# Mask and maximum of a neighbourhood attention in one VectorE instruction, and one activation table for gelu and tanh

## The chip, the cores and the metric

The kernel runs on one core of a Trainium2 chip. A core has TensorE (PE, with its weight loads shown apart), VectorE (DVE), ScalarE (ACT), GpSimd (POOL) and SyncE (SP), which issues the DMAs here. Each engine runs its own queue in order and waits for the others by semaphores. The metric is the device time of one execution in microseconds (us).

## The reference

Four layers follow one another on an input of 4 images of 128 channels, 64 x 64 pixels, all in float32: a deformable neighbourhood attention, a recurrence over the 4096 pixels, a stack of eight state-space layers (mamba), and a mixture of experts. The change lies in the first. Cut to what matters there:

```python
q = conv1x1(x, Wq, bq)
o = dwconv(q_off, off_dw_w, off_dw_b, K // 2)          # 7 x 7, by channel
o = gelu(ln2d(o, ln_w, ln_b), approximate=False)
off = tanh(einsum('bchw,oc->bohw', o, off_pw_w)) * rng
xs = grid_sample_zeros(x, off + ref)                   # offsets below one pixel
k, v = conv1x1(xs, Wk, bk), conv1x1(xs, Wv, bv)
logits = einsum('bhwgc,bhiwjgc->bhwgij', qh * SCALE, kb)   # 7 x 7 neighbours
attn = softmax(logits.reshape(B, H, W, G, K * K), -1)
out = einsum('bhwgij,bhiwjgc->bhwgc', attn, vb) + lepe
return conv1x1(out, Wo, bo)
```

The result is added to the input, and the recurrence behind it starts from a batch normalization over all of it, so it can't begin before the last block of the attention layer is done.

## The kernel before

An image is cut into 8 blocks of 512 pixels (8 rows), 32 blocks in all. A block is cut into 4 tiles of 128 queries; a tile's keys lie in a window of 14 x 22 = 308 pixels, and a mask of 0 and -1e30 leaves each query its own 7 x 7 of them. There are 4 heads to a tile.

`conv_layer` writes the order of all engines out by hand, as a software pipeline. Its loop runs over rounds `i` from -2 to 36. In a round, block `i` has the 49 taps of the 7 x 7 convolution, block `i - 1` the offset branch behind it (pieces named `o.`), block `i - 3` its attention, and blocks further back and ahead the output projection (`w.`), the next layer's first product (`v.`) and the projection to q (`q.`). Rounds 3 to 31 have both taps and attention; rounds 32 to 34 have attention without taps.

A round has 8 steps `s`, each with one pair of heads. In a step the calls are issued in this order, and each engine keeps its part of it:

1. on odd steps, PE's products with the values of the tile before (`values`); on even steps `weighed` (VectorE, L451, multiplies by the softmax's shares `ts`), the reciprocal of `share` (L423) and GpSimd's copies of the window;
2. PE transposes the two exps of the step before (`turn`, L411);
3. for each head of the pair: `masked` (VectorE, L393: logits in PSUM plus mask, to `lg` in SBUF), one tap, `largest` (VectorE, L396: the negated maximum of `lg`, to `top`), one tap, `exp` (ScalarE, L400, with `top` as its bias and the sum as its accumulator output), and `keep` (ScalarE, L419, moves a transposed exp out of PSUM);
4. on odd steps ScalarE's copies `ts` (L445) and `vk` (L374);
5. the pieces of `CPLAN`'s row left of the bar;
6. the logits of the next pair (PE, L380, two banks of PSUM, so each waits until `masked` has read the bank);
7. the rest of the step's taps;
8. `POOL_TAPS[s]` taps on ScalarE (`last_tap`: L291 multiplies, GpSimd adds in L293);
9. the pieces right of the bar.

Of the 49 taps, 39 run on VectorE (`tap`, L279; the first is L272), 3, 5, 4, 7, 6, 8, 4 and 2 of them in the eight steps. Each reads the accumulator that the one before it wrote. The other 10 run on ScalarE and GpSimd: 1 in step 1, 4 in step 4, 3 in step 5 and 2 in step 7.

In step 2 stands the offset branch: `o.norm` (L235, VectorE), `o.gelu` (L296, ScalarE), two matmuls `o.off0` and `o.off1` (L307, PE), and `o.tanh` (`fractions`: two tanh in L315, each followed by a GpSimd instruction, L316, from which the sampling of step 3 goes on). [...] Everything else in the layer uses the set with exp and ln, so `gelu` ends with a request for that set (L297) and `fractions` does too (L318); the gelu and the tanh each have a load of their own ahead of them. The profile counts these loads under L296, L297, L315 and L318.

Of the kernel before, what the change touches and what calls it, by code (L numbers as in the profile page):

```python
# [11 lines left out]
ALU = mybir.AluOpType  # L12
AX = mybir.AxisListType

EXP_LN = "natural_log_exp_and_others"
# [19 lines left out]
NKEY = KR * KC  # L35
# [75 lines left out]
CPLAN = """  # L111
w.fetch f.fetch | o.cen
o.var | o.rstd
w.rpe0 o.norm | o.gelu o.off0 o.off1 o.tanh
o.across0 | q.cen v.cen q.var o.across1 q.rstd w.rpe1
q.norm | o.down v.var w.rpe2 v.rstd
v.norm | v.pw w.wo v.wx
# [2 lines left out]
""".strip("\n").split("\n")  # L120

TAPS = 3, 5, 4, 7, 6, 8, 4, 2
POOL_TAPS = 0, 1, 0, 0, 4, 3, 0, 2
N_POOL = sum(POOL_TAPS)
NSTEP = 8


# [9 lines left out]
def conv_layer(tc, ops, I, x1_d, wx_d, stats):  # L137
# [7 lines left out]
    nc = tc.nc  # L145
    with ExitStack() as ctx:
        c = ctx.enter_context(tc.tile_pool(name="l0c", bufs=1))
        w = ctx.enter_context(tc.tile_pool(name="l0w", bufs=2))
# [18 lines left out]
        mask = c.tile([P, 9, NKEY], F32, name="mask")  # L167
        nc.sync.dma_start(out=mask, in_=I["mask"])

        def col(i):  # L170
            return vec[:, i : i + 1]
# [19 lines left out]
        scale = HD**-0.5  # L191
# [75 lines left out]
        def tap(o, t):  # L267

            x = shifted(o, t, K)
            if t == 0:  # L270
                o.acc = ps_c.tile([P, BLK], F32, tag="acc", name="acc")
                nc.vector.tensor_scalar(  # L272
                    rows(o.acc), x, dww[:, 0:1], col(V_DWB), ALU.mult, ALU.add
                )
                return
            to = o.acc
            if t == K * K - N_POOL - 1:
                to = o.off = w.tile([P, BLK], F32, tag="off", name="off")
            nc.vector.scalar_tensor_tensor(  # L279
                rows(to), x, dww[:, t : t + 1], rows(o.acc), ALU.mult, ALU.add  # L280
            )

        def last_tap(o, n):

            t = K * K - N_POOL + n
            by = dww[:, t : t + 1]
# [7 lines left out]

        def gelu(o):
            nc.scalar.activation(o.on, o.on, AF.Gelu, bias=col(V_LNB), scale=col(V_LNW))  # L296
            nc.scalar.preload_act_table_set(EXP_LN)  # L297

        def o_norm(o):
            o.on = w1.tile([P, BLK], F32, tag="on", name="on")  # L300
# [57 lines left out]
        def window(t):  # L358

            t.win = wins[t.n % len(wins)]  # L360
            nc.gpsimd.tensor_copy(
                t.win[:, 0:NKEY].rearrange("p (a b) -> p a b", a=KR),
                vt[:, t.r0 : t.r0 + KR, t.c0 : t.c0 + KC],
            )
# [23 lines left out]
        def masked(t, g):  # L388
            if g == 0:
                t.top = w.tile([P, G], F32, tag="top", name="top", bufs=3)  # L390
                t.tot = w.tile([P, G], F32, tag="tot", name="tot", bufs=3)
            t.lg[g] = w4.tile([P, NKEY], F32, tag="lg", name="lg")
            nc.vector.tensor_tensor(t.lg[g], t.pl[g][:, 0:NKEY], mask[:, t.m, :], ALU.add)  # L393

        def largest(t, g):
            nc.vector.tensor_reduce(t.top[:, g : g + 1], t.lg[g], AX.X, ALU.max, negate=True)  # L396

        def exp(t, g):
            t.ex[g] = exps[g]
            nc.scalar.activation(  # L400
                t.ex[g][:, 0:NKEY],
                t.lg[g],
                AF.Exp,
                bias=t.top[:, g : g + 1],
                accum_out=t.tot[:, g : g + 1],
            )

        def turn(t, g):
            t.pt[g] = bank("pt")
            for n in range(3):  # L410
                nc.tensor.transpose(  # L411
                    t.pt[g][:CHK, n * P : (n + 1) * P],
                    t.ex[g][:, n * CHK : (n + 1) * CHK],
                    ops.ident,
                )

        def keep(t, g):
            t.at[g] = w.tile([P, 3, P], F32, tag=f"at{g}", name="at")
            nc.scalar.copy(t.at[g][:CHK].rearrange("p n c -> p (n c)"), t.pt[g][:CHK, 0 : 3 * P])  # L419

        def share(t):

            nc.vector.reciprocal(t.tot, t.tot)  # L423
            t.rx = w.tile([P, G, HD], F32, tag="rx", name="rx")
            nc.gpsimd.tensor_copy(t.rx, t.tot.unsqueeze(2).to_broadcast([P, G, HD]))

        def values(t):

            t.pa = ps_a.tile([P, 4, P], F32, tag="pa", name="pa")
            for n in range(3):  # L430
                for g in range(G):
                    ch = slice(g * HD, (g + 1) * HD)
                    nc.tensor.matmul(
                        t.pa[ch, 0, :],
                        t.vk[:CHK, n, ch],
                        t.at[g][:CHK, n, :],
                        start=n == 0,
                        stop=n == 2,
                        skip_group_check=True,
                    )  # L440
            nc.tensor.transpose(t.pa[:, 1, :], t.rx.rearrange("p g d -> p (g d)"), ops.ident)

        def shares(t):
            t.ts = w.tile([P, P], F32, tag="ts", name="ts")
            nc.scalar.copy(t.ts, t.pa[:, 1, :])  # L445

        def weighed(t):
            o = t.block
            if t.j == 0:
                o.sblk = w.tile([P, ROWS, W], F32, tag="sblk", name="sblk")  # L450
            nc.vector.tensor_tensor(  # L451
                o.sblk[:, :, t.j * TC : (t.j + 1) * TC],
                rows(t.pa[:, 0, :]),
                rows(t.ts),
                ALU.mult,
            )
# [38 lines left out]
        def statistics(o):  # L495
# [12 lines left out]
            "o.rstd": lambda o: rstd(o, ops.eps6),  # L508
            "o.norm": o_norm,
            "o.gelu": gelu,  # L510
            "o.off0": lambda o: offset(o, 0),
            "o.off1": lambda o: offset(o, 1),
# [19 lines left out]
        plan = [[part.split() for part in row.split("|")] for row in CPLAN]  # L532
# [4 lines left out]
        def block(n):  # L537
            return blocks[n] if 0 <= n < NB else None

        def pair(p):  # L540

            if not 0 <= p < NB * NSTEP:
                return None
            t, h = divmod(p, 2)
            return tiles[t], (2 * h, 2 * h + 1)

        def tile_at(n):
            return tiles[n] if 0 <= n < len(tiles) else None
# [3 lines left out]
        for i in range(-2, NB + ATT + 2):  # L552
            who = {"q": block(i + 2), "o": block(i - 1), "w": block(i - 4), "v": block(i - 5)}
            who["f"] = block(i + 3)
            taken = n_last = 0

            def taps(n):

                nonlocal taken, n_tap
                while block(i) and n and n_tap:  # L560
                    tap(block(i), taken)
                    taken, n_tap, n = taken + 1, n_tap - 1, n - 1

            def do(what):
                if who[what[0]]:
                    pieces[what](who[what[0]])

            for s in range(NSTEP):
                p = NSTEP * (i - ATT) + s
                n_tap = TAPS[s]  # L570

                old = tile_at(p // 2 - 1) if p % 2 else None
                if old:
                    values(old)
                if p % 2 == 0:
                    if tile_at(p // 2 - 2):
                        weighed(tile_at(p // 2 - 2))
                    if tile_at(p // 2 - 1):
                        share(tile_at(p // 2 - 1))
                    if tile_at(p // 2):  # L580
                        window(tile_at(p // 2))
                now, was, then = pair(p), pair(p - 1), pair(p + 1)
                if was:
                    for g in was[1]:
                        turn(was[0], g)
                for k in range(2):
                    if now:
                        masked(now[0], now[1][k])
                        taps(1)
                        largest(now[0], now[1][k])  # L590
                        taps(1)
                        exp(now[0], now[1][k])
                    if was:
                        keep(was[0], was[1][k])
                if old:
                    shares(old)
                if p % 2 and tile_at(p // 2):
                    turn_window(tile_at(p // 2))
                for what in plan[s][0]:
                    do(what)  # L600
                if then:
                    logits(*then)
                taps(n_tap)
                for n in range(POOL_TAPS[s]):
                    if block(i):
                        last_tap(block(i), n_last)
                        n_last += 1
                for what in plan[s][1]:
                    do(what)


class Recurrence:
# [1059 lines left out]
```

## Time and profile before

| what | value |
|---|---|
| median of 3 runs | 15626.52 us (15621.09 to 15630.72) |
| the profiled execution | 15620.96 us |
| its span, from first to last instruction | 15619.2 us |
| instructions | 304876 |
| PE busy over the span | 92% |
| VectorE busy | 88% |
| ScalarE busy | 77% |
| GpSimd busy | 84% |

The attention layer takes the first 1655 us or so of the span: the last of its statistics, L496, is at 1653.46 us. The recurrence runs alone behind it (its first tanh is at 1665.71 us), and mamba from about 2000 us on; both are unchanged code. In the attention layer, from 0 to 1900 us, these groups are the ones that the change touches:

| line, engine, operation | count | mean ns |
|---|---|---|
| L393 VectorE, `lg` from `pl` and mask, 128x308 | 512 | 468 |
| L396 VectorE, `top` from `lg`, 128x308 | 512 | 468 |
| L279 VectorE, a tap, 128x512 | 1184 | 750 |
| L400 ScalarE, exp, 128x308 | 512 | 550 |
| L291 ScalarE, a tap, 128x512 | 288 | 731 |
| L293 GpSimd, its add, 128x512 | 288 | 1272 |
| L296 ScalarE, gelu, 128x512 | 32 | 813 |
| L315 ScalarE, tanh, 128x512 | 64 | 597 |
| table loads under L296, L297, L315, L318 | 32 each | 1283 |

How to read the rows below: a group's length is from its start to its last write, and the next instruction of the engine can start before that. In brackets stands how long the engine had been idle before an instruction, and what ended the wait. "xm L222 x4" is four passes over PE in one piece; a float32 matmul is counted as two. In the chain, each piece starts when what it waited for was done.

### The profile page before, as it was taken

What the parts mean: (1) busy time and instruction counts of PE and PEld (TensorE: products, weight loads), DVE (VectorE), ACT (ScalarE), POOL (GpSimd) and SP (SyncE); (2) the same over time, 40 slices, a digit from 0 to 9 for tenths busy, and PEclk for the clock granted to TensorE, in tenths of its full rate; (3) what the DMA queues carried; (4) which work ended last, traced back from release to release, by engine and by line L of the source; (5) the groups of instructions that cost most, each with busy time, mean ns of one, the idle gap of its engine ahead of it and who ended that gap; (6) DMA issues with size and microseconds to landing.
All of it is one profiled execution on the core that took longest, in us unless ns stands there. A gap on an engine that the chain in (4) does not pass through costs nothing.

```text
span 15619.2 us, 304876 instructions
## 1 busy us (share of the span) xinstructions
PE 14418.2 (92%) x121498; PEld 10710.3 (69%) x121498; DVE 13693.7 (88%) x14955; ACT 12010.6 (77%) x23617; POOL 13173.4 (84%) x9087
## 2 busy tenths in 40 slices
PE   6888989999999999999999999999999999989996
PEld 3444557777777777777777777777777777766665
DVE  8998159998999899989999899989998999999994
ACT  6888367887788788878788788878787888777773
POOL 4555059999999999999999999999999999999994
PEclk8999999999999999999999999999999999999998
DMA  0000012222222222222222222222222222222224
GB/s 22 22 22 20 18 70 105 100 97 105 100 104 96 104 96 105 99 103 99 101 102 96 104 98 105 98 105 96 103 101 103 98 98 105 96 102 94 102 94 178
DMA packets 423486, 1431.72 MB, mean 92 GB/s; under 512 B 204080, under 2 KB 204464, under 8 KB 290864
## 3 DMA queue, kind: packets, MB, share of 16 engines
q1 hardware_dynamic: 421920, 1411.95, 24.9%
q8 instruction: 960, 15.73, 0.4%
q14 instruction: 462, 3.78, 0.1%
q10 hardware_dynamic: 144, 0.26, 0.0%
HBM read 1353.33 MB, written 58.72 MB: 90 GB/s over the span
## 4 chain that ended last, share of the span: by engine, by line
POOL 62%; issue 11%; ACT 10%; PE 9%; DVE 7%; DMA 1%; POOLq 0%; SPq 0%; DVEq 0%; ACTq 0%
POOL hs L1063 46%; POOL hs L1035 6%; POOL dtx L953 4%; ACT dA L992 4%; DVE hs L1047 2%; DVE acc L279 2%; POOL state L1060 2%; POOL u L1128 2%; PE yT L1067 2%; POOL part L848 1%; PE f L865 1%; PE xm L222 1%; ACT L1147 1%; ACT xc L870 1%; PE dBx L1014 1%
## 5 line engine op out<-in xcount | busy, mean ns | idle before, releaser
L1047 DVE TENSOR_TENSOR_SCAN hs<-dA,state,dBx 128x512 f32<-128x512 f32 x7168 | 8717.6, 1263 | 987.9 <-PE dBx L1014 869.8
L1063 POOL TENSOR_TENSOR hs<-hs,Cb 128x2048 f32<-128x2048 f32 x2048 | 9293.5, 4538 | 165.8 <-POOL state L1060 1.6
L992 ACT ACTIVATE dA<-dt,A 128x512 f32<-128x512 f32 x7168 | 4729.3, 722 | 7.4 <-DVE hs L1047 1.2
L1067 PE MATMUL yT<-ident,hs 128*128 128x128 f32 x32768 | 4331.9, 276 | 8.9 <-POOL hs L1063 8.9
L1067 PEld LDWEIGHTS yT<-ident,hs 128*128 128x128 f32 x32768 | 3782.6, 144 | 770.8 <-issue 648.6
L1014 PE MATMUL dBx<-diag,dtxT 64*128 64x128 f32 x57344 | 4187.0, 286 | 72.1 <-DVE hs L1047 44.9
L1014 PEld LDWEIGHTS dBx<-diag,dtxT 64*128 64x128 f32 x57344 | 3511.7, 188 | 1026.7 <-issue 695.4
L688 ACT ACTIVATE z<-p 128x4 f32<-128x4 f32 x4096 | 710.5, 173 | 1451.6 <-PE p L685 1445.5
L685 PEld LDWEIGHTS p<-z,vt 128*128 128x128 f32 x8192 | 1233.2, 189 | 616.1 <-ACT z L688 357.1
L685 PE MATMUL p<-z,vt 128*128 128x4 f32 x8192 | 1463.2, 249 | 95.5 <-ACT z L688 78.0
L1035 POOL TENSOR_TENSOR hs<-Bb,dtx 128x512 f32<-128x512 f32 x1024 | 1274.8, 1280 | 5.7 <-PE yT L1067 4.7
L1047 DVE TENSOR_TENSOR_SCAN hs<-dAp,state,hs 128x512 f32<-128x512 f32 x1024 | 1228.4, 1262 | 0.0
L879 DVE SCALAR_TENSOR_TENSOR xc<-f,taps,xc 128x509 f32<-128x509 f32 (+2 forms) x1536 | 1130.7, 736 | 43.7 <-ACT tail L874 16.5
L980 DVE TENSOR_TENSOR diag<-f,i 128x512 f32<-128x512 f32 x1792 | 1158.2, 671 | 8.0 <-PE f L968 8.0
L1060 POOL COPY state<-hs 128x4 f32<-128x4 f32 x2048 | 387.5, 189 | 774.8 <-DVE hs L1047 617.6
L1147 ACT ACT_TABLE_LOAD x768 | 985.3, 1283 | 10.6
L279 DVE SCALAR_TENSOR_TENSOR acc<-qp,dww,acc 128x512 f32<-128x512 f32 x1184 | 887.5, 750 | 12.2
L992 ACT ACTIVATE dAp<-dt,A 128x512 f32<-128x512 f32 x1024 | 709.1, 692 | 209.4 <-DVE hs L1047 178.4
L894 PE MATMUL f<-u,given 128*128 128x512 f32 x1024 | 510.2, 620 | 333.0 <-ACT pos L1113 322.5
L870 ACT ACTIVATE xc<-f,edge,taps 128x1 f32<-128x1 f32 x1536 | 426.5, 350 | 438.9 <-POOL edge L855 438.3
L953 POOL TENSOR_TENSOR dtx<-dt,xc 128x512 f32<-128x512 f32 x512 | 651.2, 1272 | 12.1 <-ACT dt L947 12.1
L963 ACT COPY dtxT<-f 128x512 f32<-128x512 f32 x512 | 297.8, 582 | 385.3 <-PE f L960 385.3
(240 smaller groups left out, 16442.4 us busy)
## 6 DMA issues: line engine op xcount, KB each, us to landing
Cb<-c_d SPq DMA_DIRECT2D x1024, 1024.0 KB, 4.7
Bb<-c_d SPq DMA_DIRECT2D x256, 512.0 KB, 5.5
given<-in_m_given_dram SPq DMA_DIRECT2D x64, 640.0 KB, 6.0
slab<-in_w_dram SPq DMA_DIRECT2D x60, 512.0 KB, 9.9
x<-x_d SPq DMA_DIRECT2D x96, 256.0 KB, 4.8
c_d<-dbl SPq DMA_DIRECT2D x512, 32.0 KB, 1.6
x_d<-x SPq DMA_DIRECT2D x63, 256.0 KB, 2.2
xb<-in_x_dram SPq DMA_DIRECT2D x32, 256.0 KB, 3.1
```

What stands on the lines that cost most here:

```text
L279: nc.vector.scalar_tensor_tensor(rows(to), x, dww[:, t : t + 1], rows(o.acc), ALU.mult, ALU.add)
L685: nc.tensor.matmul(self.p[:, k, :], self.vt, self.before, start=False, stop=True, skip_group_check=True)
L879: nc.vector.scalar_tensor_tensor(x, o.v[h][:, : TL - k], taps[:, o.l, h, DC - 1 - k : DC - k], x, ALU.mult, ALU.add)
L953: nc.gpsimd.tensor_tensor(to, blocks(o.dt[h]), blocks(o.xc[:, h, :]), ALU.mult)
L980: nc.vector.tensor_tensor(o.diag[:, sp], bt.unsqueeze(2).to_broadcast([P, NB, 64, 2]), i64.unsqueeze(1).unsqueeze(3).to_broadcast([P, NB, ...
L992: nc.scalar.activation(o.dA[j][:, k, :], o.dt[h], AF.Exp, scale=A[:, o.l, h, n : n + 1])
L1014: nc.tensor.matmul(o.dBx[j][:, at : at + 64, :], o.dtxT[h][row, n, :], o.diag[row, sp, n], start=True, stop=True,)
L1035: nc.gpsimd.tensor_tensor(hs[:, k, :].rearrange("p (q n t) -> p q n t", n=NB, q=2), o.Bb[:, k, :].rearrange("p (q n t) -> p q n t", n=NB, ...
L1047: nc.vector.tensor_tensor_scan(hs[:, k, :], o.dA[j][:, k, :], hs[:, k, :] if sp == SP_B else o.dBx[j][:, :, k], state[:, o.l, o.b, h, s : ...
L1063: nc.gpsimd.tensor_tensor(hs, hs, o.Cb[f], ALU.mult)
L1067: nc.tensor.matmul(o.yT[:, n, :], x[:, n * P : (n + 1) * P], ops.ident, start=start and n == 0, stop=True, is_transpose=True, skip_group_c ...
L1147: return lambda o: nc.scalar.preload_act_table_set(name)
```

## The change

Mask and maximum: `masked` uses `tensor_tensor_reduce`, which writes `(pl + mask) * -1` to `lg` and the minimum of that over the 308 keys to `top`. So `top` holds the negated maximum as before, `lg` holds negated logits, and the exp takes a scale of -1. `largest` is gone, and where a tap stood ahead of it and one behind it, both taps now follow `masked`. In the built program the call is two instructions of VectorE, one that writes `lg` and one that writes `top`.

Tables: `gelu` no longer asks for the exp-and-ln set behind itself, and gelu and tanh use one set. Between `o.off1` and `o.tanh` stand two of ScalarE's ten taps (`p.tap`), one each taken from step 4 and step 5. They are the second and third of the ten in order, so each has its add on GpSimd ahead of L316. A block's loads go from four to two.

```diff
 w.fetch f.fetch | o.cen
 o.var | o.rstd
-w.rpe0 o.norm | o.gelu o.off0 o.off1 o.tanh
+w.rpe0 o.norm | o.gelu o.off0 o.off1 p.tap p.tap o.tanh
...
-POOL_TAPS = 0, 1, 0, 0, 4, 3, 0, 2
-N_POOL = sum(POOL_TAPS)
+POOL_TAPS = 0, 1, 0, 0, 3, 2, 0, 2
+N_POOL = 2 + sum(POOL_TAPS)
...
         def gelu(o):
             nc.scalar.activation(o.on, o.on, AF.Gelu, bias=col(V_LNB), scale=col(V_LNW))
-            nc.scalar.preload_act_table_set(EXP_LN)
...
-            nc.vector.tensor_tensor(t.lg[g], t.pl[g][:, 0:NKEY], mask[:, t.m, :], ALU.add)
-
-        def largest(t, g):
-            nc.vector.tensor_reduce(t.top[:, g : g + 1], t.lg[g], AX.X, ALU.max, negate=True)
+            nc.vector.tensor_tensor_reduce(
+                t.lg[g], t.pl[g][:, 0:NKEY], mask[:, t.m, :], -1.0, 3e38, ALU.add, ALU.min,
+                accum_out=t.top[:, g : g + 1],
+            )
...
                 bias=t.top[:, g : g + 1],
+                scale=-1.0,
                 accum_out=t.tot[:, g : g + 1],
...
                         masked(now[0], now[1][k])
-                        taps(1)
-                        largest(now[0], now[1][k])
-                        taps(1)
+                        taps(2)
                         exp(now[0], now[1][k])
...
-                for n in range(POOL_TAPS[s]):
-                    if block(i):
+                for what in ["p.tap"] * POOL_TAPS[s] + plan[s][1]:
+                    if what[0] != "p":
+                        do(what)
+                    elif block(i):
                         last_tap(block(i), n_last)
                         n_last += 1
-                for what in plan[s][1]:
-                    do(what)
```

## The prediction

> **What bounds the kernel now.** I read the windows by stage first, then the chain of waits inside the attention stage, then the timelines of VectorE and ScalarE along one round of it. The change touches only the convolution layer. Its last statistics feed the recurrence, so whatever the layer gains or loses reaches the end of the kernel one for one.
>
> ```profile
> 248.00:1530.00 1282.00, 1141.40 (x6358) 556.72 (x6358) 1160.22 (x2248) 1060.63 (x2322) 697.27 (x754) 0.95 0.07 22
> ```
>
> The columns are length, then PE, weight load, VectorE, ScalarE and GpSimd busy, then the granted clock. PE is busy 89%, VectorE 90%, ScalarE 83%: no engine is a bound alone, so I follow the chain. Here it is through the round from 817 to 859 us (start, length, what):
>
> ```profile
> 821.32 0.64 ACT exps L400 x2
> ...
> 822.34 1.28 ACT L296
> 823.64 0.82 ACT on L296
> 824.51 3.39 PE po L307 x4
> 827.92 0.60 ACT f L315
> 828.53 1.28 ACT L318
> ...
> 830.89 2.04 PE xm L222 x4
> ...
> 838.77 0.46 DVE lg L393
> ...
> 846.55 0.28 DVE sblk L451
> ...
> 855.34 0.29 DVE sblk L451
> ...
> 858.27 0.78 PE pl L380 x2
> ```
>
> It changes engine five times: VectorE until the maximum at 821.3 (A), ScalarE and PE for the offset branch until 829.8 (B), PE alone until the logits at 838.8 (C), VectorE until sblk at 846.6 (D), VectorE, then ScalarE, until sblk at 855.3 (E), VectorE until the bank of logits is free at 858.3 (F). After that PE again. The L296 loads at 535.04 and 965.54 us are nine rounds apart, so a round takes 47.8 us. VectorE and ScalarE in A and B:
>
> ```profile
> 818.73 0.47 DVE L396 TENSOR_REDUCE top<-lg 128x1 f32<-128x308 f32 x1
> 819.12 0.75 DVE L279 SCALAR_TENSOR_TENSOR acc<-qp,dww,acc 128x512 f32<-128x512 f32 x1
> 819.77 0.47 DVE L393 TENSOR_TENSOR lg<-pl,mask 128x308 f32<-128x308 f32 x1
> 820.16 0.75 DVE L279 SCALAR_TENSOR_TENSOR acc<-qp,dww,acc 128x512 f32<-128x512 f32 x1
> ...
> 825.96 3.12 DVE L279 SCALAR_TENSOR_TENSOR acc<-qp,dww,acc 128x512 f32<-128x512 f32 x4
> 831.95 0.29 DVE L451 TENSOR_TENSOR sblk<-pa,ts 128x128 f32<-128x128 f32 x1 [2.87 <-ACT ts L445]
> 832.15 0.17 DVE L423 RECIPROCAL tot<-tot 128x4 f32<-128x4 f32 x1
> ```
>
> ```profile
> 824.47 1.28 ACT L297 ACT_TABLE_LOAD   x1
> 825.76 1.28 ACT L315 ACT_TABLE_LOAD   x1
> 827.05 0.60 ACT L315 ACTIVATE f<-po 128x512 f32<-128x512 f32 x1
> 827.92 0.60 ACT L315 ACTIVATE f<-po 128x512 f32<-128x512 f32 x1 [0.27 <-PE po L307]
> ```
>
> Starts matter more than lengths: 819.12 less 818.73 says a maximum occupies VectorE for 0.39 us, the mask the same, and a tap between them 0.65. Four taps in a row take 3.12, 0.78 each: a tap waits for the accumulator that the tap before it wrote, and the attention instructions between taps hide that today. In B the loads L297 and L315 lie beside the two L307 matmuls (PE waits 2.46 us for the gelu first); the second tanh waits for PE, not for them.
>
> [...] the trace has 1283 and no drain (the gelu starts 1.30 us after its load), so I use 1.28. [...] The trace shows a granted 0.50 from 824.0 to 827.0, right after the 2.46 us wait; so these four passes take 3.4 us, where the same shape on a warm clock (L341) takes 2.0.
>
> **The change, part by part.** Per round 16 heads; 29 rounds have both heads and taps.
>
> *The fused instruction.* Removed per head 0.387 + 0.385 = 0.77 us of VectorE; added is a pair of price c. The main half does what L393 does (0.39, the same operands and length). For the read, the nearest small row is the reciprocal of four elements: 0.17 long, and the next instruction starts 0.085 after it. I take c = 0.475, the maximum being usable 0.39 + 0.16 + 0.03 = 0.58 us after the start. From below c is 0.39 (the read free), saving 0.085 more per head, 1.4 us a round of VectorE's work. From above: if the read waits for the whole 0.47 and holds the engine 0.19 (ScalarE's own accumulator read lasts 190 ns), c = 0.66. [...]
>
> *The taps after it.* They now come in twos, so the second waits: 0.13 us more. Counting steps of four or more taps twice, the three-tap and two-tap steps once: 14 times 0.13 = 1.8 us a round. VectorE's work falls by 16 x 0.295 - 1.8 = 2.9 us a round, but only A, D, E and F have it on the path:
> - A: today 3.62 us from the first mask to the second exp (817.70 to 821.32); after 0.475 + 0.78 + 0.65 + 0.58 = 2.49. Gain 1.13. ScalarE is free for that exp from 819.9, so it can use it.
> - D: 7.78 us today; two heads save 0.59, two new tap pairs cost 0.26. Gain 0.33.
> - E: VectorE alone would gain 0.95. But PE loses its wait of 0.51 for the mask before L341 and is otherwise without a gap to the last exp, so sblk comes about 0.4 earlier than what A to D give. Gain 0.4; the rest turns into waiting at L451.
> - F: 2.93 us become 2.83. Gain 0.1.
> - C is PE's and ScalarE's own, nothing. In step 3 and 4 VectorE's saving only lengthens its 2.87 us wait at L451.
>
> *Loads and moved taps.* Two of the four loads go, 2.57 us of ScalarE a round. Two taps (0.73 each, 0.65 back to back) come beside L307 in their place, one each out of steps 4 and 5, where ScalarE isn't on the chain: nothing there. Their two adds on GpSimd (1.27 each) now fall into its 9.7 us idle stretch before L316, and its offset work ends earlier. In B the path is L307, not the loads, whenever PE is at half clock (four passes 3.2 to 3.8 us): gelu's end to the last load takes about 4.0 both ways, no gain. In the five or so of 27 rounds where the clock is full (2.0 us), the loads decide today (3.7 us); after, L307 and a tanh do (2.6): gain 1.1. A moves the gelu 1.13 us earlier while PE's work before it stays, so PE's idle wait falls from 2.46 to 1.3 us and the half clock should come less often. The bottom is no gain at all in this respect (0.2 us a round on average), the top is full clock in every round: 4.0 less 2.6, 1.35. Rounds with a 0.98 us gap before o.cen's L222 run it at half clock in 11 of 27. I take 60% for L307, near its lower end: 0.45 us.
>
> *Scale.* The exp gets an immediate scale of -1 and the same bias: no cost, since L291 carries a scale from memory and fits the same rate. If that were wrong it would show as a longer L399.
>
> Sum: 1.13 + 0.45 + 0.33 + 0.4 + 0.1 = 2.4 us a round, 29 rounds, 70. The three rounds without taps are PE's chain save for two short stretches of heads (1565 to 1568, 1601 to 1604) and one offset branch: 3 us. The filling rounds without attention have only the loads: 2 us. Together 75. The profiled execution took 15620.96 us (its span 15619.2 and 1.8 around it), the median of the runs is 5.6 above it. 15620.96 - 75 = 15546; on the median's scale about 15550.
>
> **The rivals.**
> 1. Clock: PE stays warm at L307 everywhere, B gains 1.35, and half of o.cen's slow rounds (11 of 27 at 1.6 us more, 0.65 a round) go too: 2.4 + 0.9 + 0.5 = 3.8 us a round, with the 5 us 115: 15511. For it: the gap at L307 halves. Against it: o.cen is slow behind a gap of under 1 us.
> 2. Serial read: c = 0.66. A gains 0.87, B 0.45, E 0.35 at its last head, D and F lose 0.1 together: 1.5 a round, 46 in all: 15580. For it: nothing here shows an accumulator read on VectorE. Against it: ScalarE's starts 0.09 before its exp ends and lets the next begin after 0.09.
> 3. The other side: c = 0.97. Then VectorE has 3.2 + 1.8 = 5 us more a round and the path changes by A +0.17, B +0.45, D -0.66, E -0.9, F -0.7: 1.65 us lost a round, 48 in all: 15674. It takes the place of the gain from c = 0.81 on, and is worth 0.2% (31 us) from 0.91. [...]
>
> That the loads don't go isn't open: the order of the changed program has two a round.
>
> **How the numbers follow.** Forecast 0.60, clock 0.12, serial read 0.18, slower pair 0.10. A measurement of this kernel can tell about 0.2%, 31 us, from no change. Faster by more: 0.57 of the forecast's (0.03 could come out at under half), all of the clock's, two thirds of the serial read's: 0.81. Within: 0.03 + 0.06 + 0.02 = 0.11. Slower: 0.08. The range reaches from just beyond the clock case, 15508, to 15615, past the serial read; only the slower pair lies outside.
>
> **What would show it.** The pair's starts give c: next tap 0.45 to 0.5 us after the mask is right, above 0.8 is rival 3. Taps in twos at 0.78 and 0.65. Loads x64 in place of x128, the gap before L307's successor near 1.3 us, its passes at 3.4 or 2.0. L451's waits on ts longer. Rounds of about 45.4 us in place of 47.8, and the recurrence starting some 75 us earlier, with everything behind it unchanged. I am wrong if VectorE's saving is all waited away at L451, that is, if rounds shrink by under 1 us although c is below 0.5.

## The result, and the profile after

The changed kernel takes 15467.45 us (median of 4 runs, 15463.73 to 15478.33), the kernel before beside it 15623.81 us (4 runs, 15620.59 to 15630.72): a ratio of 0.990, 95% interval 0.9883 to 0.9918. That is 156 us gained where 75 were forecast, so the direction was right and the size half. The time lies 41 us under the range, and beyond the clock rival too.

All of it lies in the attention layer. The layer's last statistics (L496) come at 1497.00 us in place of 1653.46, 156.5 earlier. From the first tap of round 3 to that of round 31 it is 1198.86 us in place of 1344.76, 146 in 28 rounds, 5.2 a round where 2.4 were forecast. Along the stretch that the prediction read, by windows (length; PE, weight load, VectorE, ScalarE and GpSimd busy; granted clock; DMA share; GB/s), the kernel after has:

```profile
248.00:1400.00 1152.00, 1085.81 (x6425) 544.30 (x6423) 1032.35 (x2247) 980.77 (x2284) 697.21 (x759) 1.00 0.07 25
```

PE is busy 94% of it in place of 89%, VectorE still 90%, and the clock is 1.00 in place of 0.95: from 248 to 1323 us no pass of 128x512 runs at half clock any more (behind that, in the last round with taps, some do: L340's four at 1323.29 us take 3.58 in place of 1.98, and the granted clock is 0.56 from 1323.5 to 1327). The costliest groups of the layer (busy us, mean ns, then idle time ahead and what ended it):

```profile
L399 ACT ACTIVATE exps<-lg,top 128x308 f32<-128x308 f32 x512 | 283.3, 553 | 26.2 <-DVE top L392 22.1 <-POOL rx L425 1.5
...
L392 DVE CUSTOM_DVE_ANT_0 lg<-pl,mask 128x308 f32<-128x308 f32 x512 | 238.0, 468 | 39.9 <-PE pl L379 39.7
...
L392 DVE DVE_READ_ACCUMULATOR2_ANT top<- 128x1 f32 x512 | 42.3, 83 | 0.0
```

The main half of the pair is as long as the mask alone was (468 ns), the read is 83 ns, and the exp with its scale takes 553 ns against 550. VectorE's timeline in A, and ScalarE's through B (start, length, engine, line, operation):

```profile
829.48 0.47 DVE L392 CUSTOM_DVE_ANT_0 lg<-pl,mask 128x308 f32<-128x308 f32 x1
829.87 0.08 DVE L392 DVE_READ_ACCUMULATOR2_ANT top<- 128x1 f32 x1
829.87 1.54 DVE L279 SCALAR_TENSOR_TENSOR acc<-qp,dww,acc 128x512 f32<-128x512 f32 x2
```

```profile
831.01 1.28 ACT L296 ACT_TABLE_LOAD   x1
832.31 0.81 ACT L296 ACTIVATE on<-on,vec 128x512 f32<-128x512 f32 x1
833.03 1.33 ACT L291 ACTIVATE to<-qp,dww 128x512 f32<-128x512 f32 x2
834.34 0.60 ACT L314 ACTIVATE f<-po 128x512 f32<-128x512 f32 x1
835.20 0.60 ACT L314 ACTIVATE f<-po 128x512 f32<-128x512 f32 x1 [0.26 <-PE po L306]
835.81 1.28 ACT L317 ACT_TABLE_LOAD   x1
```

The read and the tap behind it start in the same instant, 0.39 us after the pair: c is 0.39, the read is free. The two taps take 1.54 as worked out (0.78 and what overlaps it). In B two loads are gone and two taps stand beside the matmuls, which PE's timeline gives:

```profile
833.18 1.98 PE L306 MATMUL po<-on,offw 128*128 128x512 f32 x4 [1.20 <-ACT on L296]
```

These four passes of the two offset matmuls (L307 before) took 3.39 us in the round that the prediction showed. Here they take 1.98, behind a wait of 1.20 in place of 2.46, and so in all 25 rounds between 266 and 1330 us. The chain of waits through the same round:

```profile
829.99 0.64 ACT exps L399 x2
...
831.01 1.28 ACT L296
832.31 0.82 ACT on L296
...
833.18 2.00 PE po L306 x4
835.20 0.60 ACT f L314
835.81 1.28 ACT L317
...
839.23 0.29 DVE sblk L451
...
845.33 0.40 DVE lg L392
...
852.58 0.28 DVE sblk L451
...
860.92 0.29 DVE sblk L451
```

C no longer ends on PE: from the sblk at 839.23 to that at 852.58 the chain stays on VectorE. A round is 42.53 us, in 24 of 25 rounds to a hundredth (the starts of L272); before it was 47.80 on average, between 46.7 and about 50.

### The profile page after: what moved, and what is told of

Read it like the earlier page. It is cut to its first block, busy times and chain, and to the rows that moved or that the text cites. A ratio compares the mean times of both kernels' runs of the same rounds, so it can differ in the third digit from the quotient of the medians.

```text
span 15476.5 us, 304793 instructions
## 1 busy us (share of the span) xinstructions
PE 14359.3 (93%) x121498; PEld 10695.0 (69%) x121498; DVE 13539.4 (87%) x14955; ACT 11916.5 (77%) x23553; POOL 13180.6 (85%) x9087
## 4 chain that ended last, share of the span: by engine, by line
POOL 62%; issue 11%; ACT 10%; PE 9%; DVE 8%; DMA 1%; POOLq 0%; SPq 0%; DVEq 0%; ACTq 0%
POOL hs L1061 46%; POOL hs L1033 6%; POOL dtx L951 4%; ACT dA L990 3%; DVE hs L1045 3%; DVE acc L279 3%; PE yT L1065 2%; POOL state L1058 2%; POOL u L1126 2%; POOL part L846 1%; PE f L863 1%; PE dBx L1012 1%; ACT xc L868 1%; ACT L1145 1%; DVE lg L392 1%
## 5 line engine op out<-in xcount | busy, mean ns | idle before, releaser
L293 POOL TENSOR_TENSOR off<-off,to 128x512 f32<-128x512 f32 x288 | 366.9, 1274 | 412.2 <-ACT to L291 399.4
```

## The experiments

Thirteen kernels. "Round" is the mean distance between two starts of the first tap (L272 before and after) over 21 to 25 rounds, read from each trace; the ratio is to runs of the kernel before on the same chip. Line numbers differ from kernel to kernel: the offset matmuls are L307, L306, L315 or L323, and o.cen's passes (`xm<-off,gcen`) are L222, L224 or L238. The texts call them L307 and o.cen.

| kernel | median us (range, runs) | ratio, 95% interval | round, us |
|---|---|---|---|
| before | 15623.81 (15620.59 to 15630.72, 4) | 1 | 47.80 |
| after | 15467.45 (15463.73 to 15478.33, 4) | 0.990 (0.9883 to 0.9918) | 42.57 |
| fused_only | 15537.68 (15533.05 to 15545.72, 4) | 0.9947 (0.9932 to 0.9962) | 44.86 |
| tables_only | 15622.32 (15616.81 to 15628.32, 12) | 1.0 (0.9991 to 1.0008) | 47.77 |
| warm | 15621.05 (15613.58 to 15628.01, 12) | 0.9999 (0.9991 to 1.0008) | 47.77 |
| warm_all | 15582.07 (15577.93 to 15590.04, 9) | 0.9973 (0.9963 to 0.9983) | 46.72 |
| tables_warm | 15547.75 (15545.53 to 15553.21, 4) | 0.995 (0.9935 to 0.9965) | 45.71 |
| extra_load | 15537.43 (15535.42 to 15544.82, 4) | 0.9949 (0.9934 to 0.9964) | 45.14 |
| fused_tables | 15516.54 (15511.24 to 15527.73, 4) | 0.9931 (0.9916 to 0.9945) | 44.34 |
| fused_4_buffers | 15528.9 (15522.84 to 15532.51, 4) | 0.9937 (0.9922 to 0.9952) | 44.80 |
| one_moved | 15460.31 (15459.13 to 15467.74, 4) | 0.9899 (0.9885 to 0.9914) | 42.57 |
| banks_of_after | 15628.9 (15621.4 to 15640.75, 12) | 1.0005 (0.9996 to 1.0014) | 48.08 |
| banks_of_before | 15490.22 (15486.43 to 15493.99, 4) | 0.9917 (0.99 to 0.9933) | 43.32 |
| fused_old_banks | 15535.72 (15529.1 to 15537.01, 4) | 0.9939 (0.9923 to 0.9956) | 44.90 |
| eleven | 15442.98 (15437.76 to 15446.29, 4) | 0.9887 (0.9872 to 0.9902) | 41.80 |

### The two parts, each alone

`fused_only` is the changed kernel without the part of the tables and the moved taps; `tables_only` is the kernel before with that part alone.

```diff
# fused_only, against the kernel after
-w.rpe0 o.norm | o.gelu o.off0 o.off1 p.tap p.tap o.tanh
+w.rpe0 o.norm | o.gelu o.off0 o.off1 o.tanh
...
-POOL_TAPS = 0, 1, 0, 0, 3, 2, 0, 2
-N_POOL = 2 + sum(POOL_TAPS)
+POOL_TAPS = 0, 1, 0, 0, 4, 3, 0, 2
+N_POOL = sum(POOL_TAPS)
...
             nc.scalar.activation(o.on, o.on, AF.Gelu, bias=col(V_LNB), scale=col(V_LNW))
+            nc.scalar.preload_act_table_set(EXP_LN)
```

> Mask and maximum in one instruction, the four loads and the ten taps as before. Theory 1 (the shorter path to the gelu is what keeps PE at full clock, and the fused instruction alone makes it shorter): L307 follows a gap of about 1.2 us and takes 2.0 us in nearly every round; with the two loads back on the path a round takes 42.5 + 1.1 = 43.6 us, the kernel about 15500. Theory 2 (the clock stays full because two loads and 2.6 us of ScalarE's work are gone): L307 stays at 3.4 us in most rounds, only the 2.0 us a round of the prediction's fused part come, about 15565.

> Shared load and moved taps, mask and maximum apart as before. Theory 1: the gap ahead of L307 stays 2.4 us and its passes slow in most rounds; only the rounds at full clock gain 1.1 us, so 0.2 to 0.4 us a round, about 15615. Theory 2: a round loses 1.1 to 1.5 us, 15580 to 15590.

The fused instruction alone gains 84 us against the kernel before on its chip, the tables with the moved taps alone nothing. Together they gain 156, so the parts don't add up: each is worth more beside the other.

In `fused_only` most rounds take 44.7 us and L307 takes 1.98 in every one of them, behind a wait of 1.20 us, although all four loads are still there: it is A, with its second exp earlier, that halves PE's wait. The clock thus went as the first theory said, but its 43.6 us a round and 15500 us were not reached. A round is 1.1 us longer than that, and the experiments on the moved taps below show why. In `tables_only` rounds of 45.71 and 49.86 us alternate; its wait is 2.4 us, and L307 and o.cen are slow in every other round. Group lines of `tables_only` and of `fused_only`, from 266 to 1330 us:

```profile
L306 PE MATMUL po<-on,offw 128*128 128x512 f32 x88 | 65.9, 890 | 53.1 <-ACT on L296 53.1
L222 PE MATMUL xm<-off,gcen 128*128 128x512 f32 x88 | 61.8, 841 | 0.0
```

```profile
L222 PE MATMUL xm<-off,gcen 128*128 128x512 f32 x96 | 47.6, 618 | 0.0
L307 PE MATMUL po<-on,offw 128*128 128x512 f32 x96 | 47.6, 618 | 28.7 <-ACT on L296 28.7
```

A pass of this shape costs 618 ns on a full clock; the means of 890 and 841 are mixtures. So this part does save time, and a slow clock takes it back. The next four kernels put a number on the clock.

### What the clock is worth

`warm` fills PE's wait ahead of L307 with nine matmuls of zeros into the bank that L307 then overwrites. `warm_all` fills two more gaps, between the two heads' logits of step 0 (four matmuls) and of step 6 (two). `tables_warm` is `tables_only` with the same three fillings.

```diff
# warm, against the kernel before
+        still = c.tile([P, P], BF16, name="still")
+        nc.gpsimd.memset(still, 0.0)
...
             o.po[ax] = bank("po")
+            if ax == 0:
+                for _ in range(9):
+                    nc.tensor.matmul(
+                        o.po[ax].rearrange("p (n t) -> p n t", n=4), still,
+                        still.unsqueeze(1).to_broadcast([P, 4, P]), start=True, stop=True,
+                    )
```

> The kernel before with nine matmuls of zeros in bfloat16 into L307's own bank ahead of it, in the gap in which PE waits for the gelu; L307 overwrites them. Theory 1: PE's clock stays full at L307 and at o.cen, all rounds become like the kernel before's fast ones, 46.7 us in place of 47.8, so about 31 us less, 15593, and the loads L297 and L315 are then the path. Rival (slow passes are a by-product, the time lies in waits elsewhere): 15620 or more.

> The kernel before with matmuls of zeros in all three of PE's gaps: nine ahead of L307, four between the two logits of step 0 (ahead of o.cen's L222), two between those of step 6. Filling L307's gap alone left 48.4 us in two rounds of three, with o.cen slow instead. Theory 1 (the clock is lost to whichever gap is left): no slow pass any more, every round 46.7 us, 15590. Rival (the clock falls for PE's low work as a whole): o.cen or another matmul stays slow, 15615 to 15625.

> The shared load and the moved taps with mask and maximum apart, and the same three fillings. Theory 1: tables_only's fast rounds of 45.7 us in every round, so the tables, worth nothing alone, give 1.0 us a round once the clock is full: 15560. Rival: no gain over the filled kernel before, 15590.

`warm` gains nothing. L307 is at full clock throughout, its wait all but filled, yet o.cen has become slow instead. Group lines of `warm`:

```profile
L224 PE MATMUL xm<-off,gcen 128*128 128x512 f32 x88 | 63.4, 862 | 0.0
...
L315 PE MATMUL po<-on,offw 128*128 128x512 f32 x88 | 43.6, 618 | 8.3 <-ACT on L298 8.3
```

Filling this one gap only moved the loss (L307 at 618 ns a pass, o.cen at 862). With all three filled every round takes 46.72 us: the clock alone is worth 47.80 - 46.72 = 1.08 us a round to the kernel before. A round of the kernel before in which no pass is slow takes the same (46.73 us). From there the two loads and the moved taps together give 46.72 - 45.71 = 1.0 more (`tables_warm`), which `tables_only` had lost to the clock.

The reverse, on the changed kernel: `extra_load` puts one load back ahead of the gelu.

```diff
+            nc.scalar.preload_act_table_set(EXP_TANH)
             nc.scalar.activation(o.on, o.on, AF.Gelu, bias=col(V_LNB), scale=col(V_LNW))
```

> The changed kernel (round 42.53 us) with a third table load put back ahead of the gelu, where the kernel before had one. The order of work stays; only PE's gap before the four passes into po (L306, 1.20 us in the changed kernel) grows by 1.28 to about 2.5. Theory 1 (the gap decides the clock, and a half-clocked PE costs about 1.1 us a round on top of the load's own time): those passes are at half speed again in at least half of the rounds (3.2 to 3.8 us for four in place of 1.98), or other passes are in their place, and the round grows by more than the load's 1.28, to 44.5 to 45.5 us: 15525 to 15555. Rival (in the changed kernel the clock stays full for another reason, such as the fuller PE elsewhere): the passes stay at 1.98 and the round grows by 1.28 at most, to 43.8: about 15505. Second rival (ScalarE isn't on the path there): no change, 15467.

The wait ahead of L307 is 2.49 us again and the time 70 us longer, in the first theory's span. The round grows by 45.14 - 42.57 = 2.57, twice the load; in the rounds where L307 stays fast it takes 43.81, which is 42.53 and the load alone. The same group of `extra_load`, and three of its rounds on PE's timeline:

```profile
L307 PE MATMUL po<-on,offw 128*128 128x512 f32 x96 | 76.3, 941 | 59.7 <-ACT on L297 59.7
```

```profile
648.10 3.08 PE L307 MATMUL po<-on,offw 128*128 128x512 f32 x4 [2.49 <-ACT on L297]
...
693.07 3.68 PE L307 MATMUL po<-on,offw 128*128 128x512 f32 x4 [2.49 <-ACT on L297]
...
738.57 1.98 PE L307 MATMUL po<-on,offw 128*128 128x512 f32 x4 [2.49 <-ACT on L297]
```

Four passes at 941 in place of 618 ns are 1.29 us; with the load's 1.28 that is the 2.57. So the load is paid for once on ScalarE and once more by PE's clock. The same wait of 2.49 gives three different lengths.

### Where the moved taps' time comes from

`fused_tables` is the changed kernel with all ten of ScalarE's taps where they were, so with the fused instruction and two loads, and no tap moved.

```diff
# against the kernel after
-w.rpe0 o.norm | o.gelu o.off0 o.off1 p.tap p.tap o.tanh
+w.rpe0 o.norm | o.gelu o.off0 o.off1 o.tanh
...
-POOL_TAPS = 0, 1, 0, 0, 3, 2, 0, 2
-N_POOL = 2 + sum(POOL_TAPS)
+POOL_TAPS = 0, 1, 0, 0, 4, 3, 0, 2
+N_POOL = sum(POOL_TAPS)
```

> The changed kernel with its ten taps of ScalarE where they were before (4 in step 4, 3 in step 5), two loads. Theory 4 (in step 4 the fourth tap waits until GpSimd has freed one of three buffers, holds up v.rstd and VectorE's tn behind it, and moving one tap away is worth about 1.2 us a round): 43.7 us a round, 15500. Rival (the moved taps are worth nothing, as was predicted, the loads 2.2 us): 42.5 us, 15467.

Its rounds take 43.68 us in some 40% and 44.85 in the others. The second kind has the products for k and v (L340) at 3.26 to 3.68 us for four passes in place of 1.98, the half clock in yet another place. So the mean, 44.34 us, and the time came out above the 43.7 and 15500 of theory 4, which the rounds at full clock meet. Against `fused_only` the two loads are worth 44.73 - 43.68 = 1.05 at full clock, about what loads and moved taps gave together in `tables_warm`. But 43.68 is still 1.15 above 42.53: that is the moved taps, which the prediction costed at nothing. The chain of `fused_only` through steps 4 and 5 shows what they stand in front of:

```profile
655.88 0.54 ACT exps L400 x2
656.42 0.37 ACT at L420
656.79 0.64 ACT to L291
657.43 0.07 issue
657.50 1.29 POOL off L293
...
658.81 0.73 ACT to L291
659.54 0.58 ACT rs L80
...
660.15 0.64 ACT rs L81
...
660.81 0.69 DVE tn L235
```

Step 4 gives ScalarE four taps, and behind them in its queue stands v.rstd (L80, L81), which VectorE's `tn` in step 5 needs. The chain passes through those taps, and here also through a GpSimd add, since the taps' buffer comes free only when that add has read it. A fourth buffer (`bufs=3` to `bufs=4` for `to`, in `fused_4_buffers`) takes that wait away:

> The fused instruction alone, four loads, all taps where they were, but four buffers for ScalarE's taps in place of three. Theory 4: the fourth tap of step 4 no longer waits for GpSimd, 0.5 to 1.2 us a round less than 44.9, 15505 to 15523. Rival (the chain there is ScalarE's own work): 15538.

It gains 9 us over `fused_only` in the median, with intervals that overlap, and next to nothing in the round (44.80 against 44.86). Its chain shows why: the add is gone from it, and ScalarE's own queue stands there in full.

```profile
702.35 0.37 ACT at L420
702.72 2.47 ACT to L291 x4
705.20 0.58 ACT rs L80
...
705.80 0.64 ACT rs L81
...
706.46 0.69 DVE tn L235
```

If this queue is the cause, one tap out of step 4 does all of it. `one_moved` moves that one alone:

```diff
# against the kernel after
-w.rpe0 o.norm | o.gelu o.off0 o.off1 p.tap p.tap o.tanh
+w.rpe0 o.norm | o.gelu o.off0 o.off1 p.tap o.tanh
...
-POOL_TAPS = 0, 1, 0, 0, 3, 2, 0, 2
-N_POOL = 2 + sum(POOL_TAPS)
+POOL_TAPS = 0, 1, 0, 0, 3, 3, 0, 2
+N_POOL = 1 + sum(POOL_TAPS)
```

> The changed kernel with only one of the two taps moved to between the loads: step 4's queue has three of ScalarE's taps as in the changed kernel, step 5's has three as before. Both moved: round 42.53. None moved: 43.68 in the rounds at full clock, 44.34 mean. Theory (ScalarE's own queue in step 4, taps ahead of v.rstd, sets the start of VectorE's tn there, and step 5's tap is off the path): all or nearly all of the 1.15 us comes with this one tap, round 42.5 to 42.8, 15467 to 15476. Rival (what counts is ScalarE's work over both steps, or GpSimd's adds behind it): about half, 43.1 at full clock, 15485. Second rival (what counts is the stretch between the loads, where the taps hold tanh or the clock): the round is near that of none moved, 15500 to 15516.

Its round is 42.52 or 42.53, that of the changed kernel. So the whole 1.15 is step 4's tap, and step 5's adds nothing. The median is 7 us lower, but its chip ran the kernel before 4 us faster too, the ranges overlap and the rounds are the same; these runs don't show the second tap to be a loss.

### The banks

The changed program releases the four PSUM banks of one pool in another order, and so hands them out in another sequence. In the kernel before the two transposes of step 4 got the same bank in 25 rounds, so the second waited until `keep` had emptied it (0.57 us, in a round of the kernel before below); in the changed kernel this never happens. The edits give each tile its bank by a fixed list, `BANKS`, a string of digits that is left out here.

```profile
837.46 0.54 PE L411 MATMUL pt<-ident,exps 128*110 128x128 f32 x3 [0.57 <-ACT at L419]
```

```diff
# banks_of_before: the kernel after with the list of before; banks_of_after: the reverse;
# fused_old_banks: fused_only with the list of before
+        order = iter(BANKS)
+
         def bank(name):
-            return ps_f.tile([P, BLK], F32, tag="f", name=name)
+            return ps_f.tile([P, BLK], F32, tag="f" + next(order), name=name, bufs=1)
```

> The kernel before, with the four PSUM banks of the shared tag handed out in the order in which the changed kernel gets them (in the kernel before, the two transposes of step 4 get the same bank in 25 rounds, in the changed one in none). Theory 3 (the handing out of banks gives 0.5 to 0.7 us a round in C): PE's wait of 0.57 us inside step 4's transposes is gone, about 15606. Rival: the wait moves to the next thing, 15624.

> The changed kernel with the four banks of its pool f handed out in the sequence of the kernel before, in which the two transposes of step 4 got the same bank in 25 rounds (PE waited 0.57 us for the copy out of it). Nothing else differs. If the new sequence is part of the gain that I left out, the round grows from 42.53 by up to 0.6 us: 15467 + 17 = 15484. If, as the kernel before with the changed sequence suggests, the wait is covered by others, the round stays within 0.1 us: 15464 to 15471.

> The fused instruction alone (round 44.73 us in most rounds, mean 44.86), but with the four banks of pool f handed out in the sequence of the kernel before. If the 2.0 us that the fused instruction brings at full clock are VectorE's, as I forecast them (A 1.13, D 0.33, E 0.4, F 0.1), the round stays at 44.7 to 44.9: 15536 to 15540. If part of them is the new sequence, which came with the changed program order and is worth 0.77 a round once VectorE is off the chain, the round grows by up to 0.8 to 45.5: up to 15560. A smaller growth, 0.1 to 0.4, would mean that the wait for the copy is partly covered by the chain through ScalarE's taps, which this kernel still has in step 4.

The new sequence alone makes the kernel before no faster. But like the tables, it does save something that the clock takes back. Where L307 alone is slow, a round takes 46.58 us on average (7 rounds) in place of 47.20 (12 rounds of before); where o.cen is slow as well, 48.58 in place of 49.28. Yet o.cen is slow in 13 of 21 rounds, where it was in 7 of 22. Its group line in `banks_of_after`, 752 ns a pass in the kernel before:

```profile
L238 PE MATMUL xm<-off,gcen 128*128 128x512 f32 x88 | 61.5, 838 | 0.0
```

No run with all gaps filled and the new sequence was made, so the size of that saving rests on like rounds alone. The old sequence costs `fused_only` nothing in the mean (44.90 against 44.86), 0.17 against its rounds at full clock (44.73). In the changed kernel the old sequence costs 43.30 - 42.53 = 0.77 us a round, 23 us in the median, more than I expected. The chain of `banks_of_before` behind the last table load is PE's, with stops:

```profile
850.68 2.59 PE po L480 x6
853.27 0.34 PE pt L427 x3
853.63 0.49 ACT at L435
854.17 0.54 PE pt L427 x3
854.71 0.72 PE pl L395 x4
```

The second transposes start only when the copy out of the first ones' bank is done, and a second stop of the same look follows 6 us later (a copy of 0.49 us at 860.49). So at most 0.17 of what the fused instruction gives is the sequence; the rest of its worth shows once everything beside PE has become earlier and the clock is full.

### A faster version

The chain of the changed kernel runs on VectorE from 839.23 to 852.58 us. `eleven` takes one tap from there and gives it to ScalarE and GpSimd in step 6.

```diff
-TAPS = 3, 5, 4, 7, 6, 8, 4, 2
-POOL_TAPS = 0, 1, 0, 0, 3, 2, 0, 2
+TAPS = 3, 5, 4, 7, 6, 7, 4, 2
+POOL_TAPS = 0, 1, 0, 0, 3, 2, 1, 2
```

> The changed kernel with one tap more taken off VectorE's step 5 (7 in place of 8) and given to ScalarE and GpSimd in step 6. In the changed kernel the chain stays on VectorE without a gap from the sblk at 839.52 us to the next at 852.58, so one tap less there should shorten it by 0.78 us: round 41.75, 29 rounds, 15467 - 22 = 15445. Rival: the tap on ScalarE in step 6 stands ahead of exps that the chain runs through (859.71 us) or v.rstd becomes the last to come again, and the round stays at 42.5 or grows by up to 0.65: 15467 to 15486. Second rival: VectorE's saving is kept but PE, busy 94% of the stage, has the rest: half, 15456.

It takes 15442.98 us, 24 less than the changed kernel and the fastest here, of which about 4 may be its chip's, where the kernel before too is 4 us faster; all of its four runs lie below all of the changed kernel's. The round is 41.82 in place of 42.53, the 0.78 forecast less 0.07. The same place of its chain:

```profile
825.85 2.59 PE po L464 x6
828.45 0.65 PE pt L411 x6
829.10 0.72 PE pl L379 x4
```

The six transposes are one piece, without a stop, and PE now sets the end of this stretch: a further tap off VectorE's step 5 should bring little. That wasn't tried.

## Why the prediction came out at half

The account of a round in us; the measured terms are differences of rounds from the kernels above:

| term | forecast | measured | from |
|---|---|---|---|
| fused instruction (A, D, E, F) | 1.96 | 1.99 | warm_all 46.72, fused_only 44.73 |
| clock, and loads (B) | 0.45 | 1.08 + 1.05 | warm_all; fused_tables at full clock 43.68 |
| moved taps | 0 | 1.15 | one_moved 42.53 |
| sum | 2.41 | 5.27 | 47.80 - 42.53 |

The measured terms are steps from one kernel to the next, so they add up by construction; in another order of steps the shares would differ. With the old sequence of banks 0.77 is lost again (`banks_of_before`): the 1.15 of the moved taps came in full only beside the new sequence.

**The fused instruction was right, in part by offsetting errors.** c is 0.39, the low end, not 0.475. So A gains 1.26 where 1.13 was forecast, and F 0.22 where 0.1 was (`fused_only`, round at 628.57 us, against the full-clock round at 474.20 of before). But C to E together gain 0.53 where D and E should have brought 0.73, because the chain there went over to ScalarE's taps. That the sum still came to 1.99 is luck, and up to 0.17 of it is the sequence of banks. The serial read and the slower pair are ruled out: both need a next tap at 0.66 us or later, where it comes at 0.39. (The slower pair's 0.97 was my estimate; no row of this case showed it.) The exp's scale cost nothing (553 against 550 ns), and the pairs of taps wait as worked out (1.54 us).

**The step that failed first is B's clock.** It was named, with its condition (A halves PE's wait ahead of L307, measured as 2.46 to 1.20) and its price, 1.35. Two choices made it small. I took 60% for the chance of a full clock behind the shorter wait, where it was every round. And I left o.cen's slow rounds as they were, where they went too. Both stood in the clock rival, 1.35 + 0.5 a round by its working, against 2.13 measured for clock and loads; it had 0.12 of the chance. (Half of o.cen's 0.65 is 0.33 and not 0.5: by its own terms the rival was 5 us smaller.) Its reason against, that o.cen is slow behind less than 1 us, treated the two places as separate, while `warm` shows a loss cured in one place coming up in another (862 ns a pass at o.cen). The experiments with and without fillers show that the terms hang together: loads and moved taps give 1.0 on a full clock and nothing without it.

**The second failure is "ScalarE isn't on the chain: nothing there".** That was read from the chain of the kernel before, where PE and VectorE end C and D. With VectorE earlier, v.rstd behind four taps is the next in line, and the prediction asked what is late next for E and L451 but not for these steps. The relief through the moved tap was worth nearly half of the whole forecast.

**C as "PE's and ScalarE's own, nothing"** missed that this part had a wait in it that the new program order happens to remove: the copy of 0.49 us at 836.93 us, between two groups of transposes, stands in the chain of the kernel before. The order of tiles in a pool was never looked at.

What is left of the 156 us: 28 rounds from the first tap of round 3 to that of round 31 gave 145.9, and the time from there to the last L496 is 10.5 shorter, of which round 31 itself should be about 5 (an estimate from the table's sum). The other 5 fell to the rounds without taps, which were given 3. The filling rounds were given 2 and brought 0.1 (the first tap of round 3 starts at 131.68 us in place of 131.76): that the two together fit is luck. Behind L496 the code is unchanged. The profiled execution stands 10.9 us above the median of the after runs.

**What stays open** is what decides at which gap the clock falls. Behind waits of 2.37 to 2.47 us the four passes of L307 took 3.2 to 3.8 us in 19 of 22 rounds of the kernel before (266 to 1330 us) and 1.98 in the other three; behind waits of 1.20 they took 1.98 in all 25 rounds read of the changed kernel and in all 24 of `fused_only`. So the length of this wait counts, but it doesn't decide alone: one of 2.49 gave 3.08, 3.68 and 1.98 us in three rounds of `extra_load`. Nor is the last wait all that counts: behind one of 0.93 us ahead of the k and v products their passes are slow (3.26 to 3.68 us for four in `fused_tables`) in three rounds of `fused_only` and in 60% of those of `fused_tables`. Why isn't shown.

## What to carry to other kernels

When several engines are each close to the end of a stretch, rank them: here steps 3 to 5 could end on VectorE, on ScalarE's queue, or on PE with a stop, within 1.2 us of each other, and an edit that shows nothing alone can be worth its full price once the one ahead of it is gone, or once the clock no longer takes its gain back (the table loads, the sequence of banks). A gap on PE cost more than its own length here (from 1.20 to 2.49 us in `extra_load`, for 2.57 a round), so price a shorter gap by the clock of all passes behind it, in every place of the round at once, and don't forecast a cure in one place while leaving the others as they were. Test a part on top of the other parts as well as alone: `tables_only` said 0, while the same loads were worth 1.05 us a round on top of the fused instruction, and one of them put back into the changed kernel cost 2.57.

## What was not expected of the hardware

- The read of VectorE's accumulator takes 83 ns and holds nothing up: the next tap, which doesn't need its result, starts with it, 0.39 us after the main instruction.
- Filling a PE wait of 2.37 to 2.47 us with matmuls (`warm`) kept the passes behind it at full clock (618 ns each), and sent other passes, fourteen microseconds ahead of them in the round, to 862 ns on average. With three gaps filled, all rounds kept the full clock (46.72 us each, where they took 47.80 on average).
- One load put back (`extra_load`) costs 1.28 us on ScalarE and, on average, 1.29 more by PE's clock.
